# Adding K's token term where M1 and M7 leave PSUM, and sending the turned maxima between a step's loads of x

## The chip, the cores and the metric

The kernel runs on one core of a Trainium2 chip. The metric is the device time of one execution in microseconds; a kernel is run several times and the median is taken. A core has five engines with a queue of instructions each: TensorE (PE; its weight loads are listed apart as PEld), VectorE (DVE), ScalarE (ACT), GpSimd (POOL) and SyncE (SP), which here only issues transfers. Instructions of one queue run in order; between queues they wait for each other by semaphores.

## The reference

Attention with a residual. The inputs are 8 sequences of 512 rows with 512 features, and one conditioning row for each sequence (`cond_1024`). Cut to what matters:

```
Q  = heads(x @ Wq.T + bq);   K  = heads(x @ Wk.T + bk);   V = heads(x @ Wv.T + bv)
tQ = heads(t @ Wq.T + bq);   tK = heads(t @ Wk.T + bk)         # t = cond[:, None, :]
scores = einsum('bhqd,bhkd->bhqk', Q + tQ, K + tK) / sqrt(32)
out = x + merge(einsum('bhqk,bhkd->bhqd', softmax(scores), V))
```

There are 16 heads of 32 features. The token's query and key (tQ, tK, with both biases in them) are one number for each feature and sequence; the kernel calls them `tok` and adds them to the projections.

## The kernel before

All arithmetic is in float32, apart from the row maxima, which are split into three bfloat16 parts. A group is four heads (128 features) of one sequence, so there are 32 groups, numbered t. After a start-up (inputs, weights turned, `tok` computed, the first groups) the main loop runs `thirds(t)` for t = 1 to 28, one step for each group, then a tail.

A step does, for group t, the exponentials and their product with V; for the groups after it, the scores whose row maxima are needed first (`row_scores`, `row_max`), and the exponentials that give the denominators; and a quarter of the next sequence's projections. The eight banks of PSUM are handed on by name (`begin`, `released`). The order on each engine is the order in which the code is written: nothing reorders it.

The projections are made of seven products M1 to M7 of half size (Strassen's scheme), in two instalments: `first` (M1, M7, M6 and half of M2) and `other` (M4, M5, the rest of M2, M3). For each half of a sequence's features (u = 0 and 1) a pair of steps makes Q, K and V:

- an odd step: Q `first` at its start, Q `other` in its middle third, K `first` in its last third;
- an even step: V `first` at its start, K `other` in its middle third, V `other` in its last third.

So K `first` and K `other` run 14 times each. Four quarters are combined in the pair tile `kT`: `c1` (with `c12` its second half) for the first of two groups, `c2` (with `c22`) for the second. K `first` is the branch `mixed is None` of `first_by_others`: VectorE copies M1 and M7 from PSUM to `c2` (L530), then adds M1 to M2 and M6 into `c1` (L531); GpSimd adds `c12` to `c22` (L533). K `other` is `other_products` with `bias`: VectorE adds M5 to `c12` (L555), then writes `c2` and `c1`, each with its token term, by `plus` (L487, a SCALAR_TENSOR_TENSOR). In the last third of the same even step TensorE computes scores of group t + 2 (`row_scores`, L641), the first to use this K; t + 2 is the first group of the pair, the one in `c1`.

In the last third of each step TensorE runs, one after another, the subtraction of maxima (L772, 4 matmuls, which read the turned maxima `maxT`), scores for the exponentials (L785, 16), scores for the row maxima (L641, 8) and the products of the next instalment (L462). An fp32 matmul shows as two passes, which is why these counts are twice those of the code.

SyncE issues in each step: stores of the results (L917, 4), four loads of a block of x (L172; VectorE turns the block at L372 one or two steps later), the transfer that turns the split maxima (L727, after GpSimd has written them at L715 to L718), swaps of kept exponentials within SBUF (L682, 2 or 6), four loads for the residual (L190), and 6 more swaps. GpSimd issues the remaining swaps (L682, POOL), before it splits the maxima. The swapped exponentials are read by the second half of L840 in the next step.

Of the kernel before, what the change touches and what calls it, by code (L numbers as in the profile page):

```python
# [9 lines left out]
F32 = mybir.dt.float32  # L10
BF16 = mybir.dt.bfloat16
AF = mybir.ActivationFunctionType
ALU = mybir.AluOpType
# [4 lines left out]
def kernel(  # L18
# [38 lines left out]
    nc = tc.nc  # L57
    P = 128
    B, S, D = x.shape
# [3 lines left out]
    HG = P // HD  # L63
    NP = HG // 2
    NS = S // P
    NC = D // P
# [7 lines left out]
    const = ctx.enter_context(tc.tile_pool(name="const", bufs=1))  # L74
# [76 lines left out]
    xs = {}  # L151
# [7 lines left out]
    BL = 32  # L159
# [3 lines left out]

        return a.rearrange("(f j) d -> j f d", j=BL)[:, :, d : d + BL]

    def load_block(n):

        b, cc = divmod(n, NC)
        if b < B:
            xs[n] = xp.tile([P, NB, BL], F32, tag="x", name=f"x_{n}")  # L170
            for h in range(HG):
                nc.sync.dma_start(xs[n][h * BL : (h + 1) * BL], spread(x[b], cc * P + h * BL))  # L172

    xr = {}
# [202 lines left out]
    def load_blocks(most=B * NC):  # L377
        for _ in range(min(most, len(to_load))):
            load_block(to_load.pop(0))
# [86 lines left out]
    def twice(a):  # L466
        return a.unsqueeze(1).broadcast_to([P, 2, HS])

    def halves(a):
        return a.rearrange("p (h s) -> p h s", h=2)  # L470
# [10 lines left out]
    def plus(n, b, u, g, o, pt, rest):  # L481

        if n == "v":
            nc.vector.tensor_tensor(o, pt, rest, ALU.add)
        else:
            add = tok[:, "qk".index(n), u * 2 + g, b : b + 1]
            nc.vector.scalar_tensor_tensor(o, pt, add, rest, ALU.add, ALU.add)  # L487
# [22 lines left out]
    def first_by_others(n, b, u, dens, at, last, mixed):  # L510

        one_, two_ = halves(banks(at[0])), halves(banks(at[1]))
        c1, c12, c2, c22 = parts_of(n, b, u)
        product(n, b, u, 1, one_[:, 0])
        product(n, b, u, 7, one_[:, 1])
        product(n, b, u, 6, two_[:, 1])
        product(n, b, u, 2, two_[:, 0], (0,))
        if mixed:
            dens((0, 1))
            nc.scalar.copy(c2, one_)  # L520
            dens((2, 3))
            nc.vector.tensor_tensor(c1, two_, twice(c2[:, 0, :]), ALU.add)
            last()
        else:
            dens((0, 1))
            if mixed is False:
                dens((2, 3))
            if mixed is None:
                dens((2, 3))
                nc.vector.tensor_copy(c2, one_)  # L530
                nc.vector.tensor_tensor(c1, two_, twice(c2[:, 0, :]), ALU.add)  # L531
                last()
                nc.gpsimd.tensor_tensor(c22, c22, c12, ALU.add)  # L533
                return
            else:
                nc.scalar.copy(c2, one_)
                nc.scalar.copy(c1, two_)
            last()
            nc.gpsimd.tensor_tensor(c12, c12, c2[:, 0, :], ALU.add)
            nc.gpsimd.tensor_tensor(c22, c22, c12, ALU.add)  # L540
            nc.gpsimd.tensor_tensor(c1[:, 0, :], c1[:, 0, :], c2[:, 0, :], ALU.add)
            return
        nc.gpsimd.tensor_tensor(c22, c22, c12, ALU.add)

    def other_products(n, b, u, dens, small, at, bias=False):

        dens()
        one_, two_ = banks(at[0]), banks(at[1])
        product(n, b, u, 4, one_[:, :HS])
        product(n, b, u, 5, one_[:, HS:])  # L550
        small()
        product(n, b, u, 2, two_[:, :HS], (1,))
        product(n, b, u, 3, two_[:, HS:])
        c1, c12, c2, c22 = parts_of(n, b, u)
        nc.vector.tensor_tensor(c12, one_[:, HS:], c12, ALU.add)  # L555
        if bias and n != "v":
            plus(n, b, u, 1, c2, halves(one_), twice(c22))
        else:
            nc.vector.tensor_tensor(c2, halves(one_), twice(c22), ALU.add)
        plus(n, b, u, 0, c1, halves(two_), c1)  # L560
        if n != "v":
            for g in range(2):
                qkT[n, b * G + u * 2 + g] = pair_of(b * G + u * 2, n)[:, g, :]
# [101 lines left out]
    def swap_kept(t, move, some=range(6)):  # L665

        later = 6 if t % 4 == 1 else 2

        def part(a, g):
            return kept[t][a * BL : (a + 1) * BL, g].rearrange("p c h s -> p (c h s)")  # L670

        for n in some:
            a, g = APART[n]
            at = (n + 2) % HG * BL
            aside = (store[:, 6:8] if t == KEPT[-1] else between)[at : at + BL, n // HG]
            aside = aside.rearrange("p i s -> p (i s)")
            to, of = [(aside, part(a, g)), (part(a, g), part(g, a)), (part(g, a), aside)][move]
            if t < KEPT[-1]:
                here = move == 2 or move == 0 and n >= later
            else:  # L680
                here = move > 0 and n >= 3
            (nc.gpsimd if here else nc.sync).dma_start(to, of)  # L682
# [39 lines left out]
    def turn_max(t):  # L722

        if t >= T:
            return
        maxT[t] = op.tile([P, S], BF16, tag="maxT", name=f"maxT_{t}")
        nc.sync.dma_start_transpose(  # L727
            maxT[t].rearrange("p (c q) -> p c q", c=NS),
            split[t % 2].rearrange("p c h e -> p (c h e)"),
        )  # L730
# [194 lines left out]

    tok = const.tile([P, 2, NC, B], F32, tag="tok", name="tok")

    part = {}

    def condition(n, pt):  # L930
# [62 lines left out]
    def turn_w(n, ccs, rows=slice(0, D)):  # L993
        for cc in ccs:
            nc.vector.transpose(wT[n][:, cc, rows], ws[n][:, cc, rows])
# [8 lines left out]
    condition_end("k", bank(0), nc.gpsimd)  # L1004
    project_qk_end(0, "k", pk)
    turn_w("v", [0])
    for cc in range(2, NC):
        project_qk_part(1, "q", cc, bank(7))
    project_qk_end(1, "q", bank(7))
# [146 lines left out]
    def thirds(t, made):  # L1156

        b, r = divmod(t, G)
        of = (t - 1) // G + 1
        begin(0, HG)  # L1160
        turn_more(t, 0, 0)
        row_max_aside(t + 1, 1)
        max_aside(t + 1, 1)
        row_max(t + 1, 2, False, HG)
        turn_more(t, 0, 1)
        denominators(t + 1, 1, None, (1, 2, 3, 0))
        denominators(t + 1, 2, HG)
        weighted(t - 1, banks(0), banks(1), nothing)
        turn_more(t, 0, 2)
        load_blocks(1)  # L1170
        one_item(of, *next(made), (2, 3), ignore, nothing)
        released(0, 1, 4, 5, 7, 6, 2, 3)
        for i in (1, 2):
            begin(HG)
            rows = (t + 1, 3) if i == 1 else (t + 2, 0)
            if i == 1:
                joined(t, i - 1, rows)
                turn_more(t, i, 0)
                row_max(*rows, False, HG, False)
            else:  # L1180
                exponentials_of_rest(t, i - 1)
                turn_more(t, i, 0)
                row_max(*rows, False, HG)
            turn_more(t, i, 1)
            if i == 1:
                first = range(6 if t + 1 < KEPT[-1] else 3)
                swap_kept(t, 2, first)
                split_max(t + 1)
                turn_max(t + 1)
                swap_kept(t, 2, range(len(first), 6))  # L1190
            dens = lambda js=range(HG): denominators(*rows, HG, js)
            n, u, kind = next(made)
            if kind == "first":
                products(of, n, u, kind, False, dens, nothing, None)
                turn_more(t, i, 2)
            elif n == "v":
                small = nothing
                if t + 1 not in KEPT:
                    small = lambda: transpose_max(t + 1, banks(2), nc.scalar.copy)
                other_shared(of, n, u, dens, (0, 3), small, lambda: turn_more(t, i, 2))  # L1200
                released(1, 2, 4, 5, 6, 7, 0, 3)
            else:
                products(of, n, u, kind, False, dens, nothing, False)
                turn_more(t, i, 2)
            if i == 1:
                aparts[t] = masked(t)
            if (t + 1, i) == (KEPT[-1], 1):
                swap_kept(t + 1, 0)
                load_residual(t + 1)
            if i == 2:  # L1210
                if r == 0:
                    combine_x(b + 1, 1, nc.gpsimd)
            else:
                if t > 1:
                    bias_residual(t)
                if r == 0:
                    combine_x(b + 1, 0, nc.gpsimd)
            if i == 2 and t + 1 < KEPT[-1]:
                swap_kept(t + 1, 0)
                load_residual(t + 1)  # L1220
                swap_kept(t + 1, 1)
# [280 lines left out]
```

## Time and profile before

| what | value |
| --- | --- |
| median of 3 runs (lowest to highest) | 649.41 us (649.35 to 650.63) |
| the profiled execution, its own time | 649.67 us |
| its span, first to last instruction | 647.8 us |
| mean granted TensorE clock | 0.999 |
| ACT busy | 533.5 us (82%) |
| POOL busy | 409.9 us (63%) |
| DMA bytes moved | 102.02 MB, mean 157 GB/s |

A row of the timeline reads: start in us from the span's start, duration in us, engine, line, operation, what it writes <- what it reads, shapes, count, and in brackets the idle time of the engine before it with what ended it. A row of the list for one line gives the least, median and greatest duration in ns and the first and last start. A row of the waits reads: who waited, on whom, us in total, times, the longest. SPq rows are SyncE's issues; a row with a count covers several instructions. Where an instruction waited for several semaphores, the one named is the one that came last by the profile.

### The profile page before, as it was taken

How to read it: one execution, taken by the hardware profiler on the slowest of the kernel's cores; microseconds unless marked ns; L12 is line 12 of the kernel's file. 1: busy time of each engine (PE TensorE's matmuls, PEld its weight loads, DVE VectorE, ACT ScalarE, POOL GpSimd, SP SyncE). 2: the span in 40 equal slices, each digit the busy share in tenths (PEclk: the TensorE clock that was granted, in tenths of full speed). 3: DMA queues.
4: the chain of work that ended last, by engine and by line, in shares of the span. 5: the costliest groups of instructions: out<-in, count | busy, mean ns of one | idle time of the engine just before them, and what ended most of it. 6: DMA issues, size and time to landing. Idle time of an engine off the chain costs nothing. (4 is left out here: it accounts for less than half of the span.)

```text
span 647.8 us, 24814 instructions
## 1 busy us (share of the span) xinstructions
PE 641.7 (99%) x9856; PEld 357.3 (55%) x9856; DVE 600.3 (93%) x845; ACT 533.5 (82%) x1364; POOL 409.9 (63%) x651
## 2 busy tenths in 40 slices
PE   9999999999999999999999999999999999999997
PEld 8445555556555555555555555555655555555541
DVE  3799999999999999999999999999999999999887
ACT  2479888889888889888888988898988888898564
POOL 3633655686765775668576776568767577675650
PEclk9999999999999999999999999999999999999999
DMA  7615588888978788877878978878898767796831
GB/s 191 107 26 85 128 164 171 172 171 191 180 158 172 161 180 175 183 165 164 185 171 174 198 150 185 165 173 169 180 195 158 156 144 163 159 189 149 192 63 34
DMA packets 248457, 102.02 MB, mean 157 GB/s; under 512 B 229962, under 2 KB 230474, under 8 KB 248340
## 3 DMA queue, kind: packets, MB, share of 16 engines
q1 hardware_dynamic: 234196, 65.54, 53.6%
q0 software_dynamic: 12384, 33.83, 20.3%
q8 instruction: 78, 1.28, 0.8%
q10 hardware_dynamic: 1760, 1.05, 0.5%
q14 instruction: 39, 0.32, 0.2%
HBM read 19.75 MB, written 8.39 MB: 43 GB/s over the span
## 5 line engine op out<-in xcount | busy, mean ns | idle before, releaser
L593 DVE TENSOR_REDUCE nmax<-psum 128x1 f32<-128x512 f32 x279 | 177.6, 675 | 9.2 <-PE psum L641 4.9
L701 ACT ACTIVATE psum<-psum,nmax 128x512 f32<-128x512 f32 x248 | 165.1, 678 | 3.6 <-DVE nmax L593 3.0
L641 PE MATMUL psum<-kT,qT 32*128 32x512 f32 x1024 | 162.0, 613 | 0.0
L701 ACT ACTIVATE store<-psum,nmax 128x512 f32<-128x512 f32 x204 | 139.5, 700 | 25.0 <-DVE nmax L593 24.8
L682 POOL DMA_DIRECT2D store<-store x258 | 128.6, 503 | 47.2 <-DMA store<-store 28.8
L799 ACT ACTIVATE store<-psum 128x512 f32<-128x512 f32 x232 | 119.8, 603 | 33.4 <-PE psum L785 33.4
L660 DVE STREAM_TRANSPOSE store<-store 128x1024 f32<-128x1024 f32 x116 | 138.9, 1217 | 0.0
L650 DVE TENSOR_REDUCE nmax<-psum 128x2 f32<-128x1024 f32 x98 | 118.9, 1213 | 0.0
L840 PE MATMUL psum<-store,v 128*32 128x256 f32 x1856 | 106.8, 381 | 0.2 <-ACT store L1320 0.2
L840 PEld LDWEIGHTS psum<-store,v 128*32 128x32 f32 x1856 | 57.3, 110 | 57.2 <-ACT wT_q L632 21.2
L913 POOL TENSOR_TENSOR res<-res,recs 128x512 f32<-128x512 f32 x30 | 31.3, 1045 | 90.8 <-DVE res L912 90.8
L785 PE MATMUL psum<-qT,kT 32*128 32x256 f32 x928 | 83.8, 374 | 0.0
L641 PEld LDWEIGHTS psum<-kT,qT 32*128 32x128 f32 x1024 | 61.6, 184 | 35.4 <-issue 17.8
L785 PEld LDWEIGHTS psum<-qT,kT 32*128 32x128 f32 x928 | 60.9, 184 | 5.6 <-issue 0.3
L701 ACT ACTIVATION_READ_ACCUMULATOR psum<-psum,nmax 128x1 f32 x248 | 55.1, 222 | 0.0
L203 POOL TENSOR_TENSOR xr<-xr,bvs 128x512 f32<-128x512 f32 x30 | 38.4, 1282 | 15.6 <-DMA x<-in_x_dram 12.8
L462 PE MATMUL psum<-wc_v,xc 128*32 128x256 f32 x768 | 47.7, 379 | 0.0
L462 PE MATMUL psum<-xc,wc_q 128*32 128x256 f32 x720 | 44.7, 379 | 0.0
L462 PE MATMUL psum<-xc,wc_k 128*32 128x256 f32 x720 | 44.5, 379 | 0.0
L701 ACT ACTIVATION_READ_ACCUMULATOR store<-psum,nmax 128x1 f32 x204 | 44.4, 217 | 0.0
L914 POOL TENSOR_TENSOR res<-res,xr 128x512 f32<-128x512 f32 x30 | 38.3, 1277 | 2.3
L462 PE MATMUL psum<-xT,wT_k 128*32 128x256 f32 x480 | 34.5, 382 | 0.0
(191 smaller groups left out, 972.5 us busy)
## 6 DMA issues: line engine op xcount, KB each, us to landing
store<-store SPq DMA_DIRECT2D x264, 128.0 KB, 2.6
store<-store POOLq DMA_DIRECT2D x258, 128.0 KB, 3.8
out_dram<-res SPq DMA_DIRECT2D x122, 64.0 KB, 3.6
xr<-in_x_dram SPq DMA_DIRECT2D x120, 64.0 KB, 4.4
x<-in_x_dram SPq DMA_DIRECT2D x112, 64.0 KB, 3.3
w_q<-in_L_cond_Wq_dram SPq DMA_DIRECT2D x4, 256.0 KB, 3.9
w_v<-in_L_cond_Wv_dram SPq DMA_DIRECT2D x16, 64.0 KB, 2.5
w_k<-in_L_cond_Wk_dram SPq DMA_DIRECT2D x16, 48.0 KB, 2.6
```

What stands on the lines that cost most here:

```text
L203: nc.gpsimd.tensor_tensor(xr[t], xr[t], bias, ALU.add)
L462: nc.tensor.matmul(pt[r], still[:, r], moving, start=(kc == kcs[0]), stop=(kc == kcs[-1]))
L593: nc.vector.tensor_reduce(nmax[t][:, qc, j : j + 1, 0], pt, AX.X, ALU.max, negate=True)
L641: nc.tensor.matmul(pt, qkT["q", t][r, qc * P : (qc + 1) * P], qkT["k", t][r, :], start=True, stop=True,)
L650: nc.vector.tensor_reduce(nmax[t][:, qc, pr * 2 : pr * 2 + 2, 0], pt, AX.X, ALU.max, negate=True)
L660: nc.vector.transpose(e, e)
L682: (nc.gpsimd if here else nc.sync).dma_start(to, of)
L701: nc.scalar.activation(to, of, AF.Exp, bias=nmax[t][:, qc, j, :], accum_out=sums[t][:, qc, j, :],)
L785: nc.tensor.matmul(banks(j)[:, i * HS : (i + 1) * HS], qkT["k", t][r, kc * P : (kc + 1) * P], qkT["q", t][r, KQ * P :], start=False, stop= ...
L799: nc.scalar.activation(e[:, j], banks(j), AF.Exp)
L840: nc.tensor.matmul(pt[j * HD : (j + 1) * HD, half * HS : (half + 1) * HS], vs[b % 2][:, kc, (g * HG + j) * HD : (g * HG + j + 1) * HD], e, ...
L914: nc.gpsimd.tensor_tensor(y, y, xr.pop(t), ALU.add)
```

## The change

Two edits.

K's token term. For K alone, `first` adds the first group's token term while it copies M1 and M7 (a TENSOR_SCALAR instead of the copy), so that all sums made of M1 carry it. In `other`, the second group's sum takes a correction `tok_left` = tok[second] - 2 tok[first] instead of its own token term, and the first group's sum needs no scalar any more: a TENSOR_TENSOR. `tok_left` is computed once in the start-up by a small VectorE instruction (`bias_left`). Q and V stay as they were.

SyncE's order. `load_block` can issue part of a block's four loads. A step issues two of them where all four were, and the two others behind the transfer of the turned maxima (`turn_max`).

```diff
-    def load_block(n):
+    def load_block(n, hs=range(HG)):
 
         b, cc = divmod(n, NC)
         if b < B:
-            xs[n] = xp.tile([P, NB, BL], F32, tag="x", name=f"x_{n}")
-            for h in range(HG):
+            if hs[0] == 0:
+                xs[n] = xp.tile([P, NB, BL], F32, tag="x", name=f"x_{n}")
+            for h in hs:
                 nc.sync.dma_start(xs[n][h * BL : (h + 1) * BL], spread(x[b], cc * P + h * BL))
...
             if mixed is None:
                 dens((2, 3))
-                nc.vector.tensor_copy(c2, one_)
+                add = tok[:, "qk".index(n), u * 2, b : b + 1]
+                nc.vector.tensor_scalar(c2, one_, add, None, ALU.add)
                 nc.vector.tensor_tensor(c1, two_, twice(c2[:, 0, :]), ALU.add)
...
         nc.vector.tensor_tensor(c12, one_[:, HS:], c12, ALU.add)
-        if bias and n != "v":
-            plus(n, b, u, 1, c2, halves(one_), twice(c22))
+        if bias and n == "k":
+            add = tok_left[:, u, b : b + 1]
+            nc.vector.scalar_tensor_tensor(
+                c2, halves(one_), add, twice(c22), ALU.add, ALU.add
+            )
+            nc.vector.tensor_tensor(c1, halves(two_), c1, ALU.add)
         else:
-            nc.vector.tensor_tensor(c2, halves(one_), twice(c22), ALU.add)
-        plus(n, b, u, 0, c1, halves(two_), c1)
+            if bias:
+                plus(n, b, u, 1, c2, halves(one_), twice(c22))
+            else:
+                nc.vector.tensor_tensor(c2, halves(one_), twice(c22), ALU.add)
+            plus(n, b, u, 0, c1, halves(two_), c1)
...
+    tok_left = const.tile([P, 2, B], F32, tag="tok_left", name="tok_left")
+
+    def bias_left():
+        nc.vector.scalar_tensor_tensor(
+            tok_left, tok[:, 1, ::2, :], -2.0, tok[:, 1, 1::2, :], ALU.mult, ALU.add
+        )
...
     turn_w("v", [0])
+    bias_left()
     for cc in range(2, NC):
...
         turn_more(t, 0, 2)
-        load_blocks(1)
+        coming = to_load.pop(0) if to_load else B * NC
+        load_block(coming, (0, 1))
         one_item(of, *next(made), (2, 3), ignore, nothing)
...
                 split_max(t + 1)
                 turn_max(t + 1)
+                load_block(coming, (2, 3))
                 swap_kept(t, 2, range(len(first), 6))
```

What stands on the engines is shown at three places. In these rows `nmax` are row maxima, `store` holds exponentials, `xT` is x turned, and lines of the kernel after are higher by 1 to 21.

VectorE at the end of an odd step, before:

```order
L660 STREAM_TRANSPOSE store<-store 128x4x256
L593 TENSOR_REDUCE nmax_1013<-psum 128x1 x2
L650 TENSOR_REDUCE nmax_1013<-psum 128x2
L530 COPY kT_1022<-psum 128x512
L531 TENSOR_TENSOR kT_1022<-psum,kT_1022 128x512
```

and after:

```order
L669 STREAM_TRANSPOSE store<-store 128x4x256
L602 TENSOR_REDUCE nmax_1015<-psum 128x1 x2
L659 TENSOR_REDUCE nmax_1015<-psum 128x2
L532 TENSOR_SCALAR kT_1024<-psum,tok 128x512
L533 TENSOR_TENSOR kT_1024<-psum,kT_1024 128x512
```

Nothing moves; the copy has become a TENSOR_SCALAR that reads `tok`.

VectorE in the middle and last third of an even step, before:

```order
L555 TENSOR_TENSOR kT_1022<-psum,kT_1022 128x256
L487 SCALAR_TENSOR_TENSOR kT_1022<-psum,tok,kT_1022 128x512 x2
L660 STREAM_TRANSPOSE store<-store 128x4x256
L593 TENSOR_REDUCE nmax_1273<-psum 128x1 x2
L650 TENSOR_REDUCE nmax_1273<-psum 128x2
L372 STREAM_TRANSPOSE xT<-x_884 128x512
L1236 TENSOR_TENSOR v_164<-psum,v_164 128x256
L1238 TENSOR_TENSOR v_164<-psum,v_164 128x2x256
```

and after:

```order
L557 TENSOR_TENSOR kT_1024<-psum,kT_1024 128x256
L560 SCALAR_TENSOR_TENSOR kT_1024<-psum,tok_left,kT_1024 128x512
L563 TENSOR_TENSOR kT_1024<-psum,kT_1024 128x512
L669 STREAM_TRANSPOSE store<-store 128x4x256
L602 TENSOR_REDUCE nmax_1275<-psum 128x1 x2
L659 TENSOR_REDUCE nmax_1275<-psum 128x2
L373 STREAM_TRANSPOSE xT<-x_886 128x512
L1257 TENSOR_TENSOR v_164<-psum,v_164 128x256
L1259 TENSOR_TENSOR v_164<-psum,v_164 128x2x256
```

The second of K's two long additions has lost its scalar; the order is the same.

SyncE over one step, before:

```order
L682 DMA store<-store 32x1024 x6
L917 DMA out_dram<-res_3531 32x16x32 x4
L172 DMA x_3542<-in_x_dram 32x16x32 x4
L727 DMA_TRANSPOSE maxT_3615<-split 128x4x128
L682 DMA store<-store 32x1024 x2
L190 DMA xr_3724<-in_x_dram 32x16x32 x4
```

and after:

```order
L691 DMA store<-store 32x1024 x6
L926 DMA out_dram<-res_3533 32x16x32 x4
L173 DMA x_3544<-in_x_dram 32x16x32 x2
L736 DMA_TRANSPOSE maxT_3615<-split 128x4x128
L173 DMA x_3544<-in_x_dram 32x16x32 x2
L691 DMA store<-store 32x1024 x2
L191 DMA xr_3726<-in_x_dram 32x16x32 x4
```

The transfer of the maxima has moved ahead of two loads, in the 22 steps that load x. The order on TensorE, ScalarE and GpSimd is the same in both kernels.

## The prediction

> **What bounds the kernel now.** I read the engines' shares first, then the steady stretch alone, then the waits of TensorE's weight loads, and then two neighbouring steps instruction by instruction.
>
> ```profile
> PE 641.7 (99%) x9856; PEld 357.3 (55%) x9856; DVE 600.3 (93%) x845; ACT 533.5 (82%) x1364; POOL 409.9 (63%) x651
> 81.00:600.00 519.00, 519.00 (x8456) 295.11 (x8451) 497.10 (x674) 454.39 (x1178) 352.77 (x581) 1.00 0.82 171
> PEld psum L641 <- ACT psum L701: 4.3, 17, 0.8
> ```
>
> In the 519 us of the steps VectorE works 497.10 us (96%) and the matmuls cover everything, at full clock (1.00). Neither has room, and they hand work to each other. A covered PE row is not yet a PE at its peak, so I look at spacing. The same passage, L785 then L641 then L462 in the last third, in an odd step (195 us) and in the next even step (214 us):
>
> ```profile
> 195.14 1.03 PE L785 MATMUL psum<-qT,kT 32*128 32x256 f32 x16
> 195.56 0.25 ACT L701 ACTIVATION_READ_ACCUMULATOR psum<-psum,nmax 128x1 f32 x1
> 195.79 0.41 PEld L641 LDWEIGHTS psum<-kT,qT 32*128 32x128 f32 x8
> 196.01 1.03 PE L641 MATMUL psum<-kT,qT 32*128 32x512 f32 x8
> 196.96 0.42 PE L462 MATMUL psum<-xT,wT_k 128*32 128x256 f32 x4
> ...
> 213.77 0.75 DVE L487 SCALAR_TENSOR_TENSOR kT<-psum,tok,kT 128x512 f32<-128x512 f32 x1 [0.17 <-PE psum L462]
> 213.81 1.03 PE L785 MATMUL psum<-qT,kT 32*128 32x256 f32 x16
> 214.23 0.25 ACT L701 ACTIVATION_READ_ACCUMULATOR psum<-psum,nmax 128x1 f32 x1
> 214.64 0.34 PEld L641 LDWEIGHTS psum<-kT,qT 32*128 32x128 f32 x8 [0.20 <-ACT psum L701]
> 214.67 1.14 PE L641 MATMUL psum<-kT,qT 32*128 32x512 f32 x8
> 215.74 0.42 PE L462 MATMUL psum<-wT_v,xc 128*32 128x256 f32 x4
> ```
>
> From L785's start to L462's start the odd step takes 196.96 - 195.14 = 1.82 us and the even one 215.74 - 213.81 = 1.93 us: TensorE loses 0.11 us there. In the odd step L641's weights begin to load 0.65 us after L785 starts, in the even one 0.83 us. The row names ScalarE, which ended at 214.23 + 0.25 = 214.48. I read it otherwise: these scores are the first to use the K that VectorE finishes at 213.77 + 0.75 = 214.52, and the load begins 0.12 us after that. So the second half of K's combination is what TensorE waits for, in each of 14 even steps; all of it is 14 x 0.11 = 1.5 us.
>
> **The change part by part.** Prices on VectorE, all from rows of the trace:
>
> ```profile
> L418 DVE TENSOR_SCALAR qT<-psum,tok x2: 751/751/751, 19.6 to 23.2; 128x512 f32<-128x512 f32 x2
> L487 DVE SCALAR_TENSOR_TENSOR kT<-psum,tok,kT x30: 484/744/751, 40.7 to 596.9; 128x512 f32<-128x512 f32 x29, 128x256 f32<-128x256 f32 x1
> L530 DVE COPY kT<-psum x14: 680/681/683, 84.5 to 582.5; 128x512 f32<-128x512 f32 x14
> L531 DVE TENSOR_TENSOR kT<-psum,kT x14: 691/692/692, 85.4 to 583.5; 128x512 f32<-128x512 f32 x14
> ```
>
> *K's second half (even steps).* The first of the two additions stays a SCALAR_TENSOR_TENSOR, with another scalar: 0. The last one, 0.75 us (the row at 213.77), becomes a TENSOR_TENSOR of the same size, 692 ns: it ends 0.06 us earlier. It starts where it did, since it waits for TensorE's product (0.17 idle). TensorE's loads of L641 can begin 0.06 us earlier, at 214.58; that is still later than the odd step's 0.65 us after L785, so the whole 0.06 counts, out of the 0.11 lost. Gain 14 x 0.059 = 0.83 us, if what comes behind lets it through. VectorE's next reduction waits for L641 and moves along. At the end of the step the row maxima wait for V's last addition, which waits for TensorE:
>
> ```profile
> 219.25 0.74 ACT L701 ACTIVATE store<-psum,nmax 128x512 f32<-128x512 f32 x1
> 219.47 0.69 DVE L1238 TENSOR_TENSOR v<-psum,v 128x512 f32<-128x512 f32 x1 [0.20 <-PE psum L462]
> 219.82 0.27 ACT L701 ACTIVATION_READ_ACCUMULATOR store<-psum,nmax 128x1 f32 x1
> 220.21 0.31 PEld L641 LDWEIGHTS psum<-kT,qT 32*128 32x128 f32 x7 [0.16 <-DVE v L1238]
> ```
>
> L1238 ends at 219.47 + 0.69 = 220.16 and the load begins 0.05 us later; moved forward by 0.06 it would still be behind ScalarE's end at 219.82 + 0.27 = 220.09, but by 0.01 only. So 0.06 us passes, and hardly more than 0.07 could: late next is ScalarE, which works without a gap from its exponentials to there.
>
> *K's first half (odd steps).* COPY, 681 ns, becomes TENSOR_SCALAR with a scalar per partition, 751 ns: 0.07 us more, 14 times, 0.98 us at most. What stands behind it:
>
> ```profile
> 199.40 0.68 DVE L530 COPY kT<-psum 128x512 f32<-128x512 f32 x1
> 200.32 0.69 DVE L531 TENSOR_TENSOR kT<-psum,kT 128x512 f32<-128x512 f32 x1 [0.24 <-ACT store L701]
> 201.06 0.31 PEld L641 LDWEIGHTS psum<-kT,qT 32*128 32x128 f32 x7 [0.22 <-DVE kT L531]
> ...
> 19.37 0.19 DVE L949 TENSOR_TENSOR tok<-sum_q,bias 128x32 f32<-128x32 f32 x1
> 19.60 0.75 DVE L418 TENSOR_SCALAR qT<-psum,tok 128x512 f32<-128x512 f32 x1
> ```
>
> TensorE waits for L531, so a later L531 would cost in full. But VectorE is idle 0.24 us between the copy's end (200.08) and L531. If that were only the time until VectorE sees its own result, it would be as short as in the start-up, where L418 reads what L949 wrote and begins 0.04 us after it. So about 0.2 us is a wait for the products in the second bank, and 0.07 fits in it: cost 0, bounded by +0.98 us if the idle time is a fixed delay and by no gain below. I take 0, the nearer by that row.
>
> *The new sum at the start.* One small instruction on VectorE between a transpose and L418, waiting for GpSimd's K sum:
>
> ```profile
> 21.83 0.24 POOL L949 TENSOR_TENSOR tok<-sum_k,bias 128x32 f32<-128x32 f32 x1 [6.10 <-DVE sum_k L943]
> 23.18 0.75 DVE L418 TENSOR_SCALAR qT<-psum,tok 128x512 f32<-128x512 f32 x1 [0.81 <-PE psum L405]
> ```
>
> GpSimd is done at 21.83 + 0.24 = 22.07, and L418 waits until 23.18 for TensorE, VectorE idle for the last 0.81 us of it. An operation of this kind (0.19 us, L949 on VectorE) lies in that: 0. Were the cover gone, it would cost its 0.2 us once.
>
> *SyncE.* Issues are the same, in another order: two loads of x, the transfer of the maxima, the two other loads.
>
> ```profile
> 214.05 4.87 SPq L172 DMA_DIRECT2D x<-in_x_dram  x4
> 215.50 0.27 POOL L718 TENSOR_TENSOR split<-rest,split 128x16 bf16<-128x16 f32 x1
> 219.03 1.21 SPq L727 DMA_TRANSPOSE maxT<-split  x1
> 221.39 5.18 SPq L682 DMA_DIRECT2D store<-store  x6
> maxT<-split SPq DMA_TRANSPOSE x29, 3.0
> 227.96 0.40 PE L772 MATMUL psum<-maxT,onesb 3*128 3x512 bf16 x4
> 228.91 0.67 DVE L372 STREAM_TRANSPOSE xT<-x 128x512 f32<-128x512 f32 x1
> SPq L682 <- DVE store L660: 38.3, 23, 5.0
> ```
>
> The maxima are ready at 215.77 and could go about 2.4 us earlier (half of 4.87). They land now at about 219.03 + 3.0 = 222.0 and are used at 227.96: 6 us early already, so nothing is gained. The two last loads go later by the transfer's issue, 1.21 us, plus what SyncE then waits for GpSimd; their issue then ends near 218.92 + 1.21 = 220.1, and with some 3 us of flight, as the transfer takes, they land near 223, before VectorE turns that block at 228.91: hidden. Behind them SyncE's swaps (L682) wait for VectorE 38.3/23 = 1.7 us a time, which covers up to 1.2 us of delay. Cost 0; bounds in the rivals.
>
> **The sum.** 0 + 0 + 0 - 0.83 us. The profiled execution took 649.67 us (span 647.8 and 1.9 around it), so 648.84; it lay 0.26 above the median of 649.41, and against that I predict 648.6 us. That is 0.13%, below the 0.2% (1.3 us) that a measurement of this kernel can tell from no change.
>
> **The rivals.**
> - *The addition isn't shorter, or ScalarE holds the load.* Speaking for it: the row names ScalarE (L701), which ends only 0.04 us before VectorE. Against it: in the odd step the same instruction ends as late after L785 starts (195.81 - 195.14 = 0.67 us; 214.48 - 213.81 = 0.67 us), and nothing is lost. Then 0 is gained: 649.4.
>   [...]
> - *The scalar operand costs on the path in odd steps.* If the 0.24 us before L531 are fixed, 14 x 0.07 = +0.98: with the gain 649.6, without it 650.4.
> - *The whole loss goes.* If the loads of L641 need only a little to catch up, 14 x 0.11 = 1.5 us: 647.9. Against it stands ScalarE's end at 220.09.
> - *Slower: the swaps come late.* SyncE issues nearly without pause; if the transfer waits for GpSimd with two loads behind it, the swaps of kept exponentials shift, and with them GpSimd's moves and the second half of L840.
>
> ```profile
> 211.51 3.02 POOL L682 DMA_DIRECT2D store<-store  x6
> 221.28 3.66 PE L840 MATMUL psum<-store,v 128*32 128x256 f32 x64
> store<-store POOLq DMA_DIRECT2D x258, 128.0 KB, 3.8
> ```
>
>   GpSimd's moves land near 211.51 + 3.02 + 3.8 = 218.3, and the second half of L840 begins near 221.28 + 1.8 = 223.1: 4.8 us of room here. It decides once SyncE lags by more than that; each step has at most 1.2 us of new delay and 1.7 us of slack to absorb it. If half of the 22 steps with loads lost 0.2 us beyond the room, 2.2 us: 651.6.
>
> **How the numbers follow.** Chances: the forecast 0.53; no gain 0.16; the scalar on the path 0.12; the whole loss gone 0.09; late swaps 0.10. Faster by over 0.2% (below 648.1): the whole loss gone and a little of the forecast's tail, 0.13. Slower (above 650.7): late swaps, 0.10. The same: 0.77. The range reaches from 647.7 (the whole loss gone) to 650.4 (the scalar without the gain) and leaves out the late swaps and some of the tails.
>
> **What the profile after would show.** The copy's place holds a TENSOR_SCALAR near 750 ns, and the addition behind it keeps its start, with 0.17 us idle before it instead of 0.24. K's last addition takes 692 ns, and the even steps' passage from L785 to L462 shrinks from 1.93 to about 1.87 us. The transfer of the maxima goes 1 to 2.5 us earlier after the first loads, and its users move no more than the rest. I am wrong if VectorE's idle time before K's second instruction stays at 0.24 us with the longer one ahead, if the passage stays at 1.93, or if a swap or L840 shows a DMA as its releaser.

## The result, and the profile after

The changed kernel took 651.82 us (median of 19 runs, 649.82 to 657.41), the kernel before 649.84 us in the same comparison (19 runs, 649.35 to 650.71): a ratio of 1.0040, 95% interval 1.0025 to 1.0054. I had forecast 648.6, 647.7 to 650.4. The change made the kernel slower, and its runs lie over 7.6 us where those of before lie over 1.4.

The profiled execution took 652.35 us. Its engine shares and its steady stretch, as shown of before:

```profile
PE 643.5 (99%) x9856; PEld 359.5 (55%) x9856; DVE 601.1 (92%) x846; ACT 534.2 (82%) x1364; POOL 409.6 (63%) x651
81.00:600.00 519.00, 518.63 (x8444) 296.04 (x8444) 495.87 (x674) 454.05 (x1179) 353.49 (x583) 1.00 0.84 171
```

The same picture: full clock, TensorE covered, VectorE at 495.87 us of 519 (497.10 before). The arithmetic does what it should. The timeline of the passage that the prediction is about, first in an odd step and then in the next even one (L794 was L785, L650 was L641, L463 was L462):

```profile
195.87 1.03 PE L794 MATMUL psum<-qT,kT 32*128 32x256 f32 x16
196.73 1.03 PE L650 MATMUL psum<-kT,qT 32*128 32x512 f32 x8
197.69 0.64 PE L463 MATMUL psum<-xT,wT_k 128*32 128x256 f32 x8
...
214.50 0.69 DVE L563 TENSOR_TENSOR kT<-psum,kT 128x512 f32<-128x512 f32 x1 [0.17 <-PE psum L463]
214.54 1.03 PE L794 MATMUL psum<-qT,kT 32*128 32x256 f32 x16
215.31 0.34 PEld L650 LDWEIGHTS psum<-kT,qT 32*128 32x128 f32 x8
215.40 1.08 PE L650 MATMUL psum<-kT,qT 32*128 32x512 f32 x8
216.41 1.07 PE L463 MATMUL psum<-wT_v,xc 128*32 128x256 f32 x16
```

K's last addition is a TENSOR_TENSOR of 0.69 us, and from L794 to L463 the even step now takes 216.41 - 214.54 = 1.87 us, 1.93 before; the odd one still 197.69 - 195.87 = 1.82. All 14 even steps of this trace take 1.87 us, where before they took 1.93 or more. The longer instruction of the odd steps and the addition behind it, from the list by line:

```profile
L532 DVE TENSOR_SCALAR kT<-psum,tok x14: 732/743/744, 85.5 to 584.5; 128x512 f32<-128x512 f32 x14
...
L533 DVE TENSOR_TENSOR kT<-psum,kT x14: 691/692/693, 86.4 to 585.4; 128x512 f32<-128x512 f32 x14
...
  ACT store L710: 2.0, 11
```

The third row is VectorE's idle time ahead of L533 as far as ScalarE ended it, us in total and times: 2.0/11 = 0.18 us. So the 0.06 us more (743 against 681 ns) were taken out of the idle 0.24. In the three other steps TensorE ended the wait (1.1 us in all); with the token edit at the old addresses, a run shown further down, it is ScalarE in all 14, 2.5/14 = 0.18 us.

What is new stands in the waits. Rows of the kernel after:

```profile
POOL store L691 <- DMA store<-store: 56.6, 48, 4.2
PEld psum L650 <- ACT psum L710: 1.6, 4, 0.8
DVE xT L373 <- DMA xr<-in_x_dram: 0.9, 1, 0.9
DVE xT L373 <- DMA x<-in_x_dram: 0.9, 1, 0.9
PE psum L849 <- DMA maxT<-split: 0.3, 1, 0.3
```

and of the kernel before:

```profile
POOL store L682 <- DMA store<-store: 28.8, 25, 2.4
```

TensorE's loads of scores wait 1.6 us in all in this row, where they waited 4.3; but in the row that names `store L710` they wait 6.2 where they waited 4.8, so the gain is to be read from the passage above and not from this row alone. GpSimd, whose moves follow SyncE's swaps, waits for those twice as long (L691 is the swaps' line), and at these lines VectorE waits twice, and TensorE once, for transfers that they did not wait for before. One such place, from the timeline after:

```profile
336.04 0.27 POOL L727 TENSOR_TENSOR split<-rest,split 128x16 bf16<-128x16 f32 x1
336.12 2.25 SPq L173 DMA_DIRECT2D x<-in_x_dram  x2
338.48 1.23 SPq L736 DMA_TRANSPOSE maxT<-split  x1
338.93 2.00 POOL L691 DMA_DIRECT2D store<-store  x4
339.75 1.73 SPq L173 DMA_DIRECT2D x<-in_x_dram  x2
346.09 0.71 DVE L373 STREAM_TRANSPOSE xT<-x 128x512 f32<-128x512 f32 x1 [0.93 <-DMA x<-in_x_dram]
```

Here SyncE begins its loads of x when GpSimd has all but split the maxima (336.04 + 0.27); in the kernel before they begin some 2 us ahead of that (rows of it stand below). It is one late step and not all of them: in the mean of the 22 steps the loads begin 1.75 us ahead of that point after the change, and 1.87 before. The last two loads are issued by 341.48 and VectorE, which waits for one of them, turns the block at 346.09, having stood 0.93 us. Where the span grew can be read from ScalarE's first copy of a step (before, then after; first and last start behind the three durations):

```profile
L632 ACT COPY wT_q<-psum x29: 585/585/587, 67.3 to 603.6; 128x512 f32<-128x512 f32 x29
```

```profile
L641 ACT COPY wT_q<-psum x29: 586/586/587, 68.3 to 605.5; 128x512 f32<-128x512 f32 x29
```

The 28 steps between took 537.2 us against 536.3. With the expected gain of 0.83 taken off, some 1.7 us were lost in them, an estimate; the start took 1.0 longer, the tail 650.6 - 605.5 = 45.1 against 44.2.

### The profile page after: what moved, and what is told of

Read it like the earlier page. It is cut to its first block, busy times and chain, and to the rows that moved or that the text cites. A ratio compares the mean times of both kernels' runs of the same rounds, so it can differ in the third digit from the quotient of the medians.

```text
span 650.6 us, 24810 instructions
## 1 busy us (share of the span) xinstructions
PE 643.5 (99%) x9856; PEld 359.5 (55%) x9856; DVE 601.1 (92%) x846; ACT 534.2 (82%) x1364; POOL 409.6 (63%) x651
## 5 line engine op out<-in xcount | busy, mean ns | idle before, releaser
L691 POOL DMA_DIRECT2D store<-store x258 | 129.0, 502 | 74.0 <-DMA store<-store 56.6
L710 ACT ACTIVATE psum<-psum,nmax 128x512 f32<-128x512 f32 x248 | 165.2, 677 | 4.4 <-DVE nmax L602 3.9
L650 PE MATMUL psum<-kT,qT 32*128 32x512 f32 x1024 | 162.0, 610 | 0.0
L710 ACT ACTIVATE store<-psum,nmax 128x512 f32<-128x512 f32 x204 | 139.7, 701 | 25.0 <-DVE nmax L602 24.5
L794 PE MATMUL psum<-qT,kT 32*128 32x256 f32 x928 | 84.1, 374 | 0.0
L650 PEld LDWEIGHTS psum<-kT,qT 32*128 32x128 f32 x1024 | 61.4, 184 | 35.5 <-issue 17.0
L794 PEld LDWEIGHTS psum<-qT,kT 32*128 32x128 f32 x928 | 60.9, 184 | 5.7 <-issue 0.3
L710 ACT ACTIVATION_READ_ACCUMULATOR psum<-psum,nmax 128x1 f32 x248 | 54.8, 221 | 0.0
L463 PE MATMUL psum<-wc_v,xc 128*32 128x256 f32 x768 | 47.7, 379 | 0.0
L463 PE MATMUL psum<-xc,wc_q 128*32 128x256 f32 x720 | 44.7, 379 | 0.0
L463 PE MATMUL psum<-xc,wc_k 128*32 128x256 f32 x720 | 44.5, 379 | 0.0
L710 ACT ACTIVATION_READ_ACCUMULATOR store<-psum,nmax 128x1 f32 x204 | 44.4, 217 | 0.0
L463 PE MATMUL psum<-xT,wT_k 128*32 128x256 f32 x480 | 34.5, 382 | 0.0
```

The lines of the kernel that those rows point to most:

```text
L463: nc.tensor.matmul(pt[r], still[:, r], moving, start=(kc == kcs[0]), stop=(kc == kcs[-1]))
L650: nc.tensor.matmul(pt, qkT["q", t][r, qc * P : (qc + 1) * P], qkT["k", t][r, :], start=True, stop=True,)
L710: nc.scalar.activation(to, of, AF.Exp, bias=nmax[t][:, qc, j, :], accum_out=sums[t][:, qc, j, :],)
L794: nc.tensor.matmul(banks(j)[:, i * HS : (i + 1) * HS], qkT["k", t][r, kc * P : (kc + 1) * P], qkT["q", t][r, KQ * P :], start=False, stop= ...
```

## The experiments

My first theory (A): SyncE's transfer, the loads behind it, the swaps and GpSimd's moves form a loop, and with two loads more in it the loop no longer fits in a step. Its rivals were the token edit (T), the mixture of transfers on the queue (D), and the moment at which the last two loads land (X).

### The two halves of the change, and the dose of loads

The token edit alone, with SyncE's order of before:

```diff
-        coming = to_load.pop(0) if to_load else B * NC
-        load_block(coming, (0, 1))
+        load_blocks(1)
...
-                load_block(coming, (2, 3))
```

> Only the token edit: SyncE issues four loads and then the transfer of the maxima, as before the change. Theory A (the time was lost because each step's transfer, two loads and swaps form a loop with GpSimd's moves that became longer than a step): 649.0 us, ratio 0.9987 (14 x 0.059 us gained), a spread as small as before's, and no wait of VectorE on a load of x and none of TensorE on the transfer of the maxima. Rival T (the token edit itself costs, by the longer instruction in odd steps): 650.4 us or more.

Measured: 653.32 us (649.8 to 659.14), ratio 1.0056 (1.0031 to 1.0080). Theory A fails: SyncE's order is that of before, and the kernel is as slow as with the whole change.

SyncE's edit alone (the copy, the additions and their scalars as before; the tile `tok_left` is still reserved):

```diff
-                add = tok[:, "qk".index(n), u * 2, b : b + 1]
-                nc.vector.tensor_scalar(c2, one_, add, None, ALU.add)
+                nc.vector.tensor_copy(c2, one_)
...
-    bias_left()
```

> Only SyncE's edit: two loads, the transfer, two loads; all arithmetic as before the change. Theory A: all of the loss and none of the gain, 652.5 us (ratio 1.004 to 1.006), a wide spread, GpSimd's issues behind the swaps waiting some 55 us in all (28.8 before), and VectorE's turn of x waiting for a load in some odd steps. Rival T: no change, 649.4.

Measured: 652.52 us (650.07 to 654.61), ratio 1.0039 (1.0025 to 1.0053). So each half alone costs about what both cost together. Neither A nor T says that.

Four loads behind the transfer:

```diff
-        load_block(coming, (0, 1))
...
-                load_block(coming, (2, 3))
+                load_block(coming)
```

> The changed kernel with the transfer of the maxima ahead of all four loads, so that four loads stand between it and the swaps. Theory A: the loop has two more loads (2.4 us) in every step and outgrows the step, so the lag is no longer caught up: 655 us or more, with the swaps late in every step. Rival X (only the moment at which the last two halves of x land counts, the swaps do not): the halves land no later than in the changed kernel by more than the time of the transfer, 652 us. Rival D (a transfer that is in flight between loads slows the queue): here it is between swaps and loads, 649 to 650 us.

Measured: 657.19 us (654.57 to 660.11), ratio 1.0119 (1.0092 to 1.0146), as A said.

Three loads, the transfer, one load:

```diff
-        load_block(coming, (0, 1))
+        load_block(coming, (0, 1, 2))
...
-                load_block(coming, (2, 3))
+                load_block(coming, (3,))
```

> The changed kernel with three loads ahead of the transfer and one behind it. Theory A: the loop has one load (1.2 us) less than in the changed kernel, so that it fits in a step nearly everywhere: 649.0 to 650.0 us and a spread smaller than the changed kernel's. Rival D (the transfer between loads slows the queue, wherever among them): 651 to 652 us.

Measured: 650.18 us (649.44 to 653.78), ratio 1.0018 (1.0005 to 1.0031). With 0, 1, 2 and 4 loads behind the transfer the medians are 653.32, 650.18, 651.82 and 657.19: not a rising line. D is out, which said 651 to 652 us with one load behind and 649 to 650 with four; so is X, which said 652 with four. The order matters, but something common to all four works besides.

What is common is a tile. `tok_left` is 2 x 8 numbers, 64 bytes a partition, and all that is laid out behind it lies 64 bytes further. In the programs as built, x begins at byte 115136 of a partition instead of 115072, xr at 146368 instead of 146304, the results (`res`) at 151104 instead of 151040, the store at 155456 instead of 155392. Behind a multiple of 256 that is 192, 192, 64 and 64, where it was 128, 128, 0 and 0. The weights, Q, K and the tile of the turned maxima move with them. A load of x or xr and a store of results moves pieces of 32 numbers, 128 bytes, and packets of under 512 bytes are 93% of all, as the profile after shows:

```profile
DMA packets 248458, 102.02 MB, mean 157 GB/s; under 512 B 229963, under 2 KB 230475, under 8 KB 248341
```

At 128 and 0 no piece crosses a multiple of 128 bytes; at 192 and 64 all do, and every second one a multiple of 256. This is theory L (place).

### The place alone

The kernel before with 64 bytes that nothing uses:

```diff
     tok = const.tile([P, 2, NC, B], F32, tag="tok", name="tok")
+    const.tile([P, 16], F32, tag="pad", name="pad")
```

> The kernel before with one tile of 64 bytes a partition that nothing uses, placed where the change placed tok_left. No instruction differs; all tiles behind it lie 64 bytes further (the store begins 64 bytes behind a multiple of 256 and no longer on one, the results too; x and xr at 192 and no longer at 128). Theory L (place: the change moved the tiles that the DMAs read and write, and the DMAs became slower): slower than before, 651.5 to 653.5 us with a spread of 4 us or more; the first step starts later than 67.35 us. Theory A (the new order of SyncE's issues) and rival T (the token edit): no change, 649.4 to 649.9.

Measured: 654.82 us (650.49 to 656.65), ratio 1.0062 (1.0038 to 1.0085). The instructions are those of before, one for one, and the engines take no longer for them at the new addresses: VectorE is busy 600.6 us (600.3 before), ScalarE 533.9 (533.5) and GpSimd 410.7 (409.9). What takes longer is in the transfers: the packets of 128 bytes took 166.5 us of 16 engines, 159.7 before, and SyncE's issuing instructions 527.6 us, 507.5 before (a table of both stands further down). The first step's start does not tell: it was 67.9 us here, but in later runs 67.3 to 68.1 whatever the place. One stretch of the timeline, before:

```profile
312.66 2.74 SPq L172 DMA_DIRECT2D x<-in_x_dram  x4
314.48 0.27 POOL L718 TENSOR_TENSOR split<-rest,split 128x16 bf16<-128x16 f32 x1
315.51 1.22 SPq L727 DMA_TRANSPOSE maxT<-split  x1
323.52 0.10 PEld L772 LDWEIGHTS <-onesb 3*128 3x128 bf16 x4 [0.41 <-issue]
323.53 0.40 PE L772 MATMUL psum<-maxT,onesb 3*128 3x512 bf16 x4
```

and with the 64 bytes:

```profile
316.61 4.28 SPq L172 DMA_DIRECT2D x<-in_x_dram  x4
316.72 0.28 POOL L718 TENSOR_TENSOR split<-rest,split 128x16 bf16<-128x16 f32 x1
321.00 1.48 SPq L727 DMA_TRANSPOSE maxT<-split  x1
324.67 0.10 PEld L772 LDWEIGHTS <-onesb 3*128 3x128 bf16 x4 [0.98 <-DMA maxT<-split]
324.67 0.40 PE L772 MATMUL psum<-maxT,onesb 3*128 3x512 bf16 x4 [0.50 <-DMA maxT<-split]
```

SyncE begins its loads 4.0 us later than before and the transfer 5.5 us later (0.6 of it are the later start); the maxima, which landed early before, land too late, and TensorE waits 0.98 us with its weights and 0.50 with the product. It is one of two such steps in this trace; in the others the maxima land in time.

### The change without the moved tiles

The 64 bytes laid into the sums of the condition for Q, which are dead by then; all other addresses as before:

```diff
-            add = tok_left[:, u, b : b + 1]
+            add = sum4s["q"][:, u, b : b + 1]
...
-    tok_left = const.tile([P, 2, B], F32, tag="tok_left", name="tok_left")
+    sum4s = {}
...
-            tok_left, tok[:, 1, ::2, :], -2.0, tok[:, 1, 1::2, :], ALU.mult, ALU.add
+            sum4s["q"][:, :2], tok[:, 1, ::2, :], -2.0, tok[:, 1, 1::2, :], ALU.mult, ALU.add
...
-        sum4 = const.tile([P, NC, B], F32, tag=f"sum4{n}", name=f"sum4_{n}")
+        sum4 = sum4s[n] = const.tile([P, NC, B], F32, tag=f"sum4{n}", name=f"sum4_{n}")
```

With the token edit alone:

> The token edit alone, with its 64 bytes laid into a tile that is no longer needed (the sums of the condition for Q), so that every other tile has the address it has before the change. Theory L: the gain of K's shorter last addition and nothing else, 648.8 to 649.1 us (ratio 0.9987), and a spread as small as before's. Rival T: as slow as the run of the token edit alone, 652 to 653 us.

Measured: 648.54 us (648.15 to 649.61), ratio 0.9980 (0.9972 to 0.9989).

With the whole change:

> The whole change, with its 64 bytes in that same tile, so that all addresses are as before. Theory L in its pure form: 648.8 to 649.1 us, since the order of SyncE's issues costs nothing once the DMAs are as fast as before. Theory A: 651 us or more, since the loads behind the transfer still lengthen SyncE's loop with GpSimd. Both at work: in between, 649.5 to 650.5 us.

Measured: 648.68 us (647.98 to 649.36) beside 650.02 for before, ratio 0.9980 (0.9971 to 0.9989). That meets the forecast of 648.6, and it is a version that beats both kernels. Both runs lie a little below the 648.8 to 649.1 expected: the gain came out at 0.2%, where 0.83 us are 0.13%. SyncE's order costs nothing here: 648.68 with it, 648.54 without.

With the transfer ahead of all four loads:

> The transfer ahead of all four loads, all addresses as before. With the 64 bytes in a tile of their own this order took 657.2 us, the changed kernel 651.8 to 652 and the order of before 653.3. Theory L in its pure form: 649 to 650 us. Theory A with L: 653 to 655 us: slower than before, but less than with the moved tiles.

Measured: 649.80 us (648.42 to 651.71), ratio 0.9998 (0.9989 to 1.0006): some 1.1 us more than the changed order. So the order can cost something, as theory A says, but it needs four loads behind the transfer to show 1.1 us; with the moved tiles the same order took 657.19. Whether that works by the loop that A supposes is not shown. GpSimd waits 56.1 us for the swaps in this run, as long as in the changed kernel (56.6), and the run loses nothing against the kernel before: that wait marks a late SyncE, and by itself it is not the loss.

### Which tiles

The store alone 64 bytes further, in the kernel before:

```diff
+    EB.tile([P, 16], F32, tag="pad", name="pad")
     store = EB.tile([P, 18, 2, S], F32, tag="eb", name="store")
```

> The kernel before with 64 unused bytes a partition directly ahead of the store: the store alone lies at 64 behind a multiple of 256, and x, xr and the results where they were. Theory S (the swaps within the store are what became slower, so that their loop with GpSimd lags): as slow as the run with all tiles moved, 652 to 655 us. Theory R (the loads into x and xr and the transfers out of the results became slower, in pieces of 128 bytes): no change, 649.4 to 650.2 us. Half and half: 650.5 to 651.5.

Measured: 650.02 us (649.54 to 650.70) beside 649.84, ratio 1.0004 (0.9996 to 1.0013): no change.

All but the store 64 bytes further (the unused tile in `tok_left`'s place, and a small tile at the end of the pool taken out so that the store stays):

> The kernel before with x, xr and the results (and weights, Q and K) 64 bytes further and the store where it was. Theory S: no change, 649.4 to 650.2 us. Theory R: 652 to 655 us. [...]

Measured: 651.87 us (650.08 to 655.84), ratio 1.0031 (1.0017 to 1.0045). So the loads of x and xr or the stores of results carry a loss without the store being moved, and the store alone carries none. All of it together lost more (1.0062, 1.0038 to 1.0085); whether the store adds to the loss of the others is open. The wait of GpSimd on the swaps grows with all but the store moved. Rows of all-but-the-store, then of the store alone, then of the whole change at the old addresses:

```profile
POOL store L683 <- DMA store<-store: 56.3, 53, 2.4
```

```profile
POOL store L683 <- DMA store<-store: 29.6, 28, 2.1
```

```profile
POOL store L691 <- DMA store<-store: 32.2, 33, 2.4
```

The packets of SyncE's queue took longer (queue, packets, MB, share of the span of 16 engines), before, after, and with all but the store moved:

```profile
q1 hardware_dynamic: 234196, 65.54, 53.6%
```

```profile
q1 hardware_dynamic: 234196, 65.54, 55.1%
```

```profile
q1 hardware_dynamic: 234196, 65.54, 54.5%
```

With the spans 647.8, 650.6 and 650.5 us that is 347.2, 358.5 and 354.5 us of all 16 engines: the same packets, 2 to 3% slower. (In the run with 64 unused bytes it is 351.6, 1% more; the runs at the old addresses lie between 342 and 348.) The traces hold each packet, and added up by size they say which ones: the 198,144 packets of 128 bytes took 159.7 us before, 169.1 after and 167.8 with all but the store moved, 5 to 6% more; the 8,448 packets of 4 KB, which are SyncE's swaps, took 149.5, 149.8 and 148.7. So the swaps' own packets are not slower; what stands ahead of them in the queue is.

128 unused bytes instead of 64 (x and xr now on a multiple of 256, the results and the store 128 behind one):

```diff
+    const.tile([P, 32], F32, tag="pad", name="pad")
```

> The kernel before with 128 unused bytes in the place of tok_left: x and xr now start on a multiple of 256 (128 behind one before), the results and the store 128 behind one (on one before). No piece of 128 bytes crosses a multiple of 128. If only such crossings matter: no change, 649.4 to 650.2 us. If the start of the store's rows on a multiple of 256 matters: 651.5 to 655 us.

Measured: 649.81 us (649.24 to 650.52), ratio 1.0001 (0.9993 to 1.0010): no change. So it is not that things move: 64 bytes cost (ratio 1.0062) and 128 do not, as theory L says of pieces that cross. Anything else that depends on an address being a multiple of 128 would look the same here.

The whole change, with every one of these tiles starting on a multiple of 256 (one tile for both sums of the condition, 128 bytes unused ahead of the results):

> The whole change with its 64 bytes in an older tile, and besides x and xr moved so that they too start on a multiple of 256, as the results and the store do. If the place of x and xr within 256 bytes matters: 647.5 to 648.4 us, and fewer us of GpSimd's waits for the swaps. If not: 648.5 to 648.9 us as with the change at the old addresses.

Measured: 648.72 us (648.20 to 649.17), ratio 0.9983 (0.9975 to 0.9992): as with x and xr 128 behind one. Nothing more shows.

The results alone, and the loads alone, 64 bytes further (unused tiles ahead of `res`; or ahead of x, with the results back on a multiple of 256 and the store 128 behind one, and with the weights, Q, K and the maxima's tile moved like x):

> The kernel before with the results' tiles alone 64 bytes further, so that every second piece of 128 bytes that goes out of them crosses a multiple of 128 and 256; x, xr and the store where they were. If the transfers out of the results carry the loss: 651.5 to 653 us. If the loads into x and xr carry it: 649.4 to 650.2. If each carries half: 650.3 to 651.2 us.

Measured: 650.52 us (649.82 to 651.93), ratio 1.0014 (1.0005 to 1.0023).

> The kernel before with x and xr (and the weights, Q and K) 64 bytes further, the results on a multiple of 256 as before, and the store 128 behind one, which cost nothing in the run with 128 bytes. If the loads into x and xr carry the loss: 651.5 to 653 us. If the transfers out of the results do: 649.4 to 650.2. If each carries half: 650.3 to 651.2 us.

Measured: 649.97 us (649.73 to 651.24) beside 649.84, ratio 1.0009 (1.0000 to 1.0018). The results' part is shown; the loads' lies at the edge of its interval and, alone, in the range that I had expected if the results carry it all. Together (1.0031) they cost more than the sum of the two (1.0023), but the intervals allow either. Two sums over the traces go the same way, the packets of 128 bytes and the time that SyncE's issuing instructions took (one trace of each kernel, SyncE's order as before):

| 64 bytes further | packets of 128 bytes, us of 16 engines | SyncE issuing, us | ratio |
| --- | --- | --- | --- |
| nothing | 159.7 | 507.5 | 1 |
| the store | 160.1 | 507.0 | 1.0004 |
| x and xr (loads) | 161.3 | 507.3 | 1.0009 |
| the results | 164.3 | 517.2 | 1.0014 |
| x, xr and results | 167.8 | 523.8 | 1.0031 |
| all | 166.5 | 527.6 | 1.0062 |
| all, by 128 bytes | 160.1 | 506.1 | 1.0001 |

With the results moved the packets take longer and SyncE's instructions with them; with the loads alone the packets hardly do (161.3 us against 159.7 to 161.2 at the old addresses), and the instructions do not (507.3 us against 507.5). Why the loads cost more beside moved results is open.

What it is in a transfer that pays for the place, no run shows; that it is the crossing of a multiple of 128 or 256 bytes is theory L, which these runs do not tell from other causes. They show the price: 64 bytes behind a multiple of 256 the results cost 1.0014, 128 behind one nothing (1.0001), and the store with its rows of 4 KB shows no cost at 64 either (1.0004). The results are read by their transfers, x and xr are written to; whether both pay in the same way the runs don't tell.

## Why the prediction was wrong, point by point

- *K's second half:* right. The passage went from 1.93 to 1.87 us, as forecast, in all 14 even steps, and at the old addresses the whole change gains 650.02 - 648.68 = 1.34 us (interval 0.7 to 1.9), which holds the 0.83 forecast. That 648.68 lies so near 648.6 is in part luck: the kernel before stood at 650.02 in that comparison, not at the 649.41 from which I had counted, and the gain is larger by 0.5 than the term that I can show.
- *K's first half:* right. The idle time ahead of L533 fell from 0.24 to 0.18 us where ScalarE ends it. The rival that the scalar operand costs on the path is out, and so is that of no gain.
- *SyncE's order:* cost 0, right at the old addresses (648.68 against 648.54); there the transfer began 0.4 us behind the end of the split in the mean of the 22 steps, where it began 1.6 us behind it before: 1.2 us earlier, within the 1 to 2.5 forecast. That "each step has at most 1.2 us of new delay and 1.7 us of slack to absorb it" was still a poor sum, since 1.7 us is the mean of 23 waits, some of them shorter, and what a step doesn't absorb can be carried to the next; with four loads behind the transfer 1.1 us were lost.
- *The new sum at the start:* this step failed. I costed its instruction ("An operation of this kind ... lies in that: 0") and not its tile. The tile's 64 bytes move all that lies behind it, so that the pieces of x, xr and the results cross multiples of 128 bytes: in the kernel before the move alone costs 4.0 us by the ratio of 1.0062 (2.5 to 5.5), and the whole change the difference between 1.0040 and 0.9980, 3.9 us. The diff showed the tile, and the trace showed that the path of its harm was tight: SyncE's issuing instructions alone take 507.5 of the 647.8 us.
- *Late swaps* (651.6, a chance of 0.10) had the right sign and picture, swaps late and DMAs as releasers, but not the cause: I put it down to the order, and it needs the slower transfers (358.5 us of 16 engines on SyncE's queue, 347.2 before): at the old addresses the same order costs nothing (648.68 against 648.54). That its 651.6 lies next to the measured 651.82 is luck. The sign that I named for it, a DMA as releaser of a swap, was no sign either: the profile before has it already (28.8 us), and only its size changed.

The wide spread of the changed kernel belongs to the same cause: at the old addresses its runs lie over 1.4 us. I take it that how late SyncE gets differs from run to run, and the steps that stall with it; that isn't shown, since each kernel has one trace.

Open is why the medians at the moved addresses don't rise evenly with the loads behind the transfer (653.32, 650.18, 651.82, 657.19). One thing stands beside it: in seven of the longest runs (four of the 12 with the token edit alone, two with four loads behind the transfer, one with 64 unused bytes) the granted clock was 0.995 or 0.996, and 0.998 or more in every other run. By that share a clock lower by 0.003 makes some 2 us of 650, an estimate; whether the late transfers bring it on isn't shown. And 1.0 us of the profiled execution's longer start is not explained by the place: that start was 67.3 us with all but the store moved, and 68.0 with the change at the old addresses:

```profile
L633 ACT COPY wT_q<-psum x29: 585/585/586, 67.3 to 605.8; 128x512 f32<-128x512 f32 x29
```

```profile
L641 ACT COPY wT_q<-psum x29: 585/585/591, 68.0 to 603.2; 128x512 f32<-128x512 f32 x29
```

## What to carry to other kernels

A new tile can have a price beyond its instruction: this one moved the tiles laid out behind it, and with transfers in pieces of 128 bytes the shift by 64 cost more (1.0062 in the kernel before) than the edit gains (0.9980). Before judging an edit, compare where the tiles lie, and lay small additions into dead space (648.68 us for this change, 651.82 with a tile of its own) or round them to 128 bytes (128 unused bytes: 1.0001). When two unrelated halves of a change each cost what the whole costs, look for what both have in common; a kernel with an unused tile in the same place settles it in one run.

## What the runs showed of the hardware

I had not expected that 64 bytes in the place of a tile are worth 0.3 to 0.6% (others 1.0031, all 1.0062), while 128 bytes are worth nothing (1.0001), nor that rows of 4 KB, moved alone, don't mind (1.0004). Results that lie 64 bytes behind a multiple of 256 went, in one trace of each kernel, with 3% more time in packets of 128 bytes (164.3 against 159.7 us) and 2% more in SyncE's issuing (517.2 against 507.5 us). Nor had I expected that, where the packets of SyncE's queue take 1 to 3% longer in all (351.3 to 358.5 us of 16 engines against 347.2, one trace each), a kernel with 1.4 us between its slowest and fastest run becomes one with 4 to 9 us.
